# An attention and feed-forward layer on one core: the order of early loads, of one normalization and of the sums of Wq

## The chip, the core and the metric

The kernel runs on one core of a Trainium2 chip. A core has a matrix engine (TensorE, PE in the profile), three engines for elementwise work (VectorE or DVE, ScalarE or ACT, GpSimd or POOL) and SyncE (SP), which here only issues transfers. Each engine works off its own queue in order. A transfer is issued by an instruction in the queue of SP, ACT or POOL and then runs on 16 DMA engines that all queues share. The metric is the device time of one execution in microseconds (us).

## The reference

Everything is float32. There are 16 rows of a batch, each 128 by 1024.

```python
def layernorm(x):                       # over the last axis, no gain, no bias
    return (x - mean(x)) / sqrt(var(x) + 1e-5)

q = layernorm(x) @ Wq + bq              # 1024 -> 1024: 32 heads of 32
k = ctx @ Wk + bk                       # 1024 -> 256:  8 heads of 32
v = ctx @ Wv + bv                       # 1024 -> 256
w = softmax(q k^T / sqrt(32))           # four heads of q share one of k and v
x = x + (w v) @ Wo + bo                 # 1024 -> 1024
e = layernorm(x); e[:, 819:] *= -4      # the last fifth is inhibitory
out = x + scale * (e @ kernel)          # kernel: 1024 x 1024 of zeros and ones
```

## The kernel before, in words

**Groups and steps.** The 16 rows of the batch make 8 groups of two (`GB = 2`). A group's attention takes four steps; in a step `attend` (L761) issues the scores of one row and half of the heads as 32 small matmuls, and then for each of four tiles a maximum (`negm`, VectorE), four exponentials (ScalarE), a division (`inv` and `p`, VectorE), four transpositions (`tpp`, TensorE) and a copy (`pt`, ScalarE). At its end `weighted` (L606) multiplies by v. Between these parts TensorE works on the dense matmuls of the neighbouring groups.

**The order is written out by hand.** Under `tc.manual_schedule()` (L830) every instruction goes into its engine's queue in the order in which the program issues it. `Stream` (L23) makes this order: it keeps a clock `now`, a list of generators that issue dense work in pieces and tell how long each takes (about 0.85 us), and events that `later(us, fn)` puts at a time on that clock. `run` issues the events that are due, then the next piece. The clock is only the program's own reckoning; on the chip each instruction starts when its queue and its operands let it.

**Weights come in pieces.** Wq and Wo stay in memory and pass through a ring of eight pieces of 512 KB (`fetch`, L220). From the second group on, both products are made with seven block products in place of eight (`seven`, L462). They need four sums of blocks of Wq and four of Wo, which `combine` (L782) makes in place from the loaded pieces, one half of 128 by 512 at a time (L796), and stores to memory (L799); later fetches read them back. `spread` (L805) issues one sum every so many us of the clock. The sums of the second half of Wq and both halves of Wo run on GpSimd, those of the first half of Wq on VectorE.

**The start.** Ahead of the hand-written part the contexts of rows 0 and 1, Wv, Wk and the rows 0 and 1 of x are loaded (L186 to L191), the first ones over the queues of SP, ACT and POOL in turn. `load_by_quadrants` (L155) takes its queues in rotation; Wk is cut in two halves of four transfers, eight transfers of 128 KB in all. Then SP issues six pieces of Wq, the contexts of rows 2 and 3, two more pieces, the four blocks of Wo of `load_o_part(0)` (L816, issued at L823), and the rows 2 and 3 of x (`load_x`, L166, issued at L169). TensorE meanwhile makes v and k of the first group, transposes the normalized rows 0 and 1, and begins q with `plain(0)`, which uses the pieces as they are, without sums.

**Step one and two of the first group.** TensorE goes on with `plain(1)`, 16 pieces of q in four groups of four, during step one, and with k and v of the second group during step two. `norms(nxt, 8.5, 25.0)` puts the normalization of row 2 at 8.5 us and that of row 3 at 25.0 us on the stream's clock after the scores of step one. A normalization (`norm_x`, L387) is, on VectorE, two statistics (L283), their aggregate (L287), an addition (L289) and the scaling `xn` (L292), and between the last two one power on GpSimd (`rs_a`, L291). `between(gen, n, fn)` (L920) calls `fn` after the n-th piece of a generator; here it starts the sums of the first half of Wq, one every 1.5 us of the clock. `sums_of_wq(1)` starts those of the second half on GpSimd, one every 3.3 us. The four sums of Wo were started before step one (`sums_of_wo`, L867), also one every 3.3 us. When the last sum of a half is issued, its stores and four fetches follow on SP.

Of the kernel before, what the change touches and what calls it, by code (L numbers as in the profile page):

```python
# [76 lines left out]
def once(fn, *args):  # L77
    fn(*args)
    yield 0.0
# [3 lines left out]
def kernel(  # L83
# [71 lines left out]
    def load_by_quadrants(dst, w, queues, *cuts):  # L155

        src = w.rearrange("(k c f) n -> k f c n", k=NB, f=32)
        n = 0
        for lo, hi in zip((0,) + cuts, cuts + (NC,)):
            for k in range(NB):  # L160
                queues[n % len(queues)].dma_start(
                    out=dst[k * 32 : (k + 1) * 32, lo:hi], in_=src[k][:, lo:hi]
                )
                n += 1

    def load_x(b, tag="row"):  # L166

        x_t = work.tile([P, D], FP, tag=tag, name=f"xn{b}", bufs=2)
        nc.sync.dma_start(out=x_t, in_=x[b])  # L169
        xns[b] = x_t  # L170
# [11 lines left out]

    three = (nc.sync, nc.scalar, nc.gpsimd)
    load_ctx(0, three)  # L186
    load_by_quadrants(wv_sb, Wv, (nc.scalar, nc.gpsimd, nc.sync), 2, 4)
    load_ctx(1, three)
    load_by_quadrants(wk_sb, Wk, (nc.scalar, nc.gpsimd, nc.sync), 4)
    load_x(0)  # L190
    load_x(1)  # L191
    ident = const.tile([P, P], FP, name="ident")
# [27 lines left out]
    def fetch():  # L220
        n = len(pieces)
        if n < len(feed):
            t = work.tile([P, PIECE], FP, tag="piece", name=f"piece{n}", bufs=RING)
            src = feed[n]()
            nc.sync.dma_start(out=t.rearrange("p (c n) -> p c n", c=src.shape[1]), in_=src)
            pieces.append(t)
# [603 lines left out]
    with tc.manual_schedule():  # L830
        stream = Stream()

        at_q = {}
        for k in range(2):
            for o in range(2):
                for r in range(2):
                    at_q[r, o, k] = want(lambda r=r, o=o, k=k: q_block(r, o, k))
        qs, os = {1: prep_q(1)}, {}
        for grp in range(NGRP):
            os[grp] = out_proj(grp)  # L840
            if grp + 2 < NGRP:
                qs[grp + 2] = prep_q(grp + 2)

        for _ in range(RING - 2):
            fetch()
        for j in range(GB):
            load_ctx(GB + j)
        for _ in range(2):
            fetch()
        o_parts = [load_o_part(0)]  # L850
        for j in range(GB):
            load_x(GB + j, "turn")

        def plain(a):
            return prep_q_plain(a, {(r, k): at_q[r, a, k] for r in range(2) for k in range(2)})

        for j in range(GB):
            for h in range(2):
                turn_ctx(j, h)
            stream.add(prep_v(0, [j]))  # L860
        stream.add(prep_k(0))
        stream.run(0.0, lambda: len(stream.queue) > 1)
        nc.vector.tensor_scalar_mul(bqs, bqT, scale)
        for j in range(GB):
            norm_x(j)

        def sums_of_wo():  # L867
            def then():
                o_parts.append(load_o_part(1))

            stream.later(10.0, load_ffn)
            stream.later(8.0, lambda: spread(combine("o", 0, o_parts[0]), 3.3, then))

        stream.add(
            prep_x(0, 0),
            prep_x(0, 1),
            once(sums_of_wo),
            once(prep_ctx, 1, 7.0, 9.0, 11.0, 12.0),
            plain(0),
        )  # L880
        stream.run(0.0, lambda: stream.queue)

        def norms(grp, *us):
            for j in range(GB):
                stream.later(us[j], lambda j=j: norm_x(grp * GB + j))

        def get_x(grp):

            for j in range(GB if grp < NGRP else 0):
                b = grp * GB + j  # L890
                load_x(b, "turn")
                stream.later((10.0 if grp == 2 else 5.0) + 4.0 * j, lambda b=b: rows_x(b))

        def turn_rows(grp):
            for n, at in enumerate((30.0, 32.0, 34.0, 36.0)):
                stream.later(at, lambda n=n: turn_x(grp * GB + n // 2, n % 2))

        def get_ctx(grp):
            if grp < NGRP:
                for j in range(GB):  # L900
                    load_ctx(grp * GB + j)

        def residuals(grp):
            for j in range(GB):
                load_residual(grp * GB + j, 1.0 if grp == 0 else 4.0)

        def sums_of_wq(k):
            def then():
                for _ in range(4):
                    fetch()  # L910
                if k == 1:
                    spread(combine("o", 1, o_parts[1]), 3.3)

            part = {(r, o): pieces[at_q[r, o, k]] for r, o in BLOCKS}
            if k == 0:
                spread(combine("q", k, part, nc.vector), 1.5, then)
            else:
                spread(combine("q", k, part), 3.3, then)

        def between(gen, n, fn, *args):  # L920

            for i, us in enumerate(gen):
                yield us
                if i + 1 == n:
                    fn(*args)

        for grp in range(NGRP):
            b0, b1, nxt = grp * GB, grp * GB + 1, grp + 1
            p0, p1 = b0 - 2, b0 - 1
            first, more = grp == 0, nxt < NGRP  # L930
            last = grp == NGRP - 1
            length = 17.4 if first else 23.2 if grp < NGRP - 2 else 19.2
            if first:
                stream.add(
                    once(norms, nxt, 8.5, 25.0),
                    between(plain(1), 9, sums_of_wq, 0),
                    once(sums_of_wq, 1),
                    prep_k(nxt),
                    once(get_ctx, nxt + 1),
                    prep_v(nxt),  # L940
                    prep_x(nxt, 0),
                    prep_x(nxt, 1),
                    once(convert_ffn),
                    between(qs[nxt], 40, residuals, grp),
                )
            elif more:
                stream.add(
                    *([once(get_x, nxt), once(prep_ctx, nxt, 3.7, 8.0, 13.0, 18.0)] if grp == 1 else []),
                    once(turn_rows, nxt),
                    os[grp - 1],  # L950
                    once(get_ctx, nxt + 1),
                    prep_k(nxt),
                    once(load_residual, b0, 4.0),
                    prep_v(nxt),
                    qs[nxt],
                    once(get_x, nxt + 1),
                    once(prep_ctx, nxt + 1, 2.5, 7.0, 11.0, 16.0),
                )

                if nxt < NGRP - 1:  # L960
                    stream.add(ffn(p0), once(load_residual, b1, 2.0), ffn(p1))
            else:
                stream.add(
                    once(load_residual, p1, 1.0, "ctx"),
                    os[grp - 1],
                    once(load_residual, b0, 4.0, "ctx"),
                    ffn(p0 - 2),
                    once(load_residual, b1, 4.0),
                    ffn(p1 - 2),
                )  # L970
            if not more:
                for q in range(2 * NA):
                    b, a = grp * GB + q % GB, q // GB
                    start = stream.now
                    pts = attend(b, a, 15.0)
                    stream.later(15.0, lambda b=b, a=a, pts=pts: weighted(b, a, pts) or 1.0)
                    stream.run(start + 12.0)
                stream.run(stream.now, lambda: (b, a) not in yTs)
                break
            for q in range(2 * NA):  # L980
                b, a = grp * GB + q % GB, q // GB
                start = stream.now
                pts = attend(b, a, length)
                if q == 2 * NA - 1:
                    stream.run(start + length - 2.0, lambda: stream.queue)
                else:
                    stream.run(start + length - 2.0)
                stream.run(stream.now, lambda: None in pts)
                weighted(b, a, pts)
                stream.now += 1.0  # L990
        stream.add(
            os[NGRP - 1],
            ffn(B - 4),
            mixed(ffn(B - 3), ffn_transpose(B - 2), 10, 2),
            mixed(ffn(B - 2), ffn_transpose(B - 1), 8, 2),
            ffn(B - 1),
        )
        stream.drain()
# [49 lines left out]
```

## Time and profile before

| what | us |
|---|---|
| three timed runs | 785.81, 786.40, 787.71 (median 786.4) |
| the profiled execution | 785.56 |
| its span, first to last instruction | 783.8 |
| scores of step one, two, three begin | 41.58, 61.95, 80.50 |
| TensorE busy from 41.6 to 61.9 | 17.98 of 20.30 |
| TensorE busy from 61.9 to 80.5 | 18.11 of 18.60 |
| TensorE busy from 200 to 700 | 500 of 500 |
| TensorE idle before its first matmul | 7.01 |

The granted TensorE clock is 1.00 in all of these stretches. In a timeline a row gives the start, the duration, the engine, the line of the program, the operation, what it writes and reads, the shapes and the number of instructions that are merged in it; in brackets stands the idle time of the engine before it, and what ended it. A small q behind an engine's name (SPq, ACTq) is its queue issuing a transfer. Engines read ahead, so that a row can start a little before the one above it ends.

### The profile page before, as it was taken

The page shows a single profiled execution, that of the slowest core. Times are in us where ns is not written, and L with a number is a line of the kernel's source. Part 1 is how long each engine was busy: PE and PEld are TensorE (multiplying, and loading weights), DVE is VectorE, ACT ScalarE, POOL GpSimd, SP SyncE. Part 2 cuts the span into 40 slices and gives each one's busy share as a digit, 9 for nine tenths or more (in the row PEclk, how much of TensorE's full clock was granted, in tenths as well). Part 3 has the DMA queues.
Part 4 walks back from the last instruction along what each step waited for, and adds up shares of the span by engine and source line. Part 5 has one row for each costly group of instructions (what it writes and reads, how often), then busy time and mean ns, then how long its engine had stood idle before and what let it go on. Part 6 is the DMA issues. An engine that isn't in the chain of part 4 may idle for free.

```text
span 783.8 us, 13740 instructions
## 1 busy us (share of the span) xinstructions
PE 765.3 (98%) x5008; PEld 570.7 (73%) x5008; DVE 488.7 (62%) x887; ACT 323.1 (41%) x1261; POOL 114.6 (15%) x142
## 2 busy tenths in 40 slices
PE   5999999999999999999999999999999999999997
PEld 4877884689747986479855898558985689456476
DVE  1358648756766667466784667755676666765552
ACT  0244854435234453344433444344434445575100
POOL 4066502010100102020020200202001010103000
PEclk9999999999999999999999999999999999999999
DMA  9999899969698777878688795977769667763702
GB/s 241 317 332 316 327 342 372 271 196 304 236 299 237 235 237 233 293 215 262 222 270 264 192 290 207 307 230 206 265 216 313 207 199 235 253 202 103 264 27 81
DMA packets 99412, 192.42 MB, mean 245 GB/s; under 512 B 8256, under 2 KB 57728, under 8 KB 99344
## 3 DMA queue, kind: packets, MB, share of 16 engines
q1 hardware_dynamic: 97568, 189.30, 75.4%
q10 hardware_dynamic: 1248, 1.11, 0.6%
q0 software_dynamic: 528, 1.12, 0.6%
q8 instruction: 40, 0.66, 0.4%
q14 instruction: 28, 0.23, 0.1%
HBM read 161.09 MB, written 30.41 MB: 244 GB/s over the span
## 4 chain that ended last, share of the span: by engine, by line
PE 87%; DMA 6%; DVE 4%; POOL 1%; issue 1%; SPq 0%; ACT 0%; DVEq 0%; POOLq 0%
PE f L323 14%; PE o_u L662 13%; PE q_u L451 13%; PE o_v L662 7%; PE tpp L601 7%; PE q_v L451 7%; PE v L323 6%; PE k L323 5%; PE sc L568 4%; PE av L611 4%; PE q_c L451 3%; PE o_c L662 3%; DMA ctx<-in_ctx_dram 2%; DMA wo<-in_L_xattn_Wo_dram 1%; DMA piece<-in_L_xattn_Wq_dram 1%; POOL wo L796 1%
## 5 line engine op out<-in xcount | busy, mean ns | idle before, releaser
L584 ACT ACTIVATE p<-sc,negm 128x128 f32<-128x128 f32 x512 | 181.4, 369 | 133.2 <-DVE negm L580 73.1
L603 ACT COPY pt<-tpp 128x512 f32<-128x512 f32 x128 | 74.7, 591 | 146.8 <-PE tpp L601 146.5
L580 DVE TENSOR_REDUCE negm<-sc 128x4 f32<-128x512 f32 x128 | 86.8, 680 | 45.6 <-PE sc L568 45.6
L584 ACT ACTIVATION_READ_ACCUMULATOR p<-sc,negm 128x1 f32 x512 | 105.5, 206 | 0.0
L323 PE MATMUL f<-wf_sb,x2l 128*128 128x512 f32 x256 | 104.3, 407 | 0.0
L323 PE MATMUL f<-wf_sb,x2h 128*128 128x512 f32 x256 | 100.5, 393 | 0.0
L596 DVE TENSOR_TENSOR p<-p,inv 128x512 f32<-128x512 f32 x128 | 91.9, 718 | 4.4
L451 PE MATMUL q_u<-t,piece 128*128 128x128 f32 x672 | 81.3, 275 | 0.0
L601 PEld LDWEIGHTS tpp<-ident,p 128*128 128x128 f32 x512 | 61.9, 141 | 24.6 <-issue 16.7
L601 PE MATMUL tpp<-ident,p 128*128 128x128 f32 x512 | 75.9, 273 | 3.4 <-DVE p L596 3.2
L451 PEld LDWEIGHTS q_u<-t,piece 128*128 128x128 f32 x672 | 78.1, 192 | 0.1
L180 POOL TENSOR_TENSOR x<-x,bo_b 128x256 f32<-128x256 f32 x64 | 54.3, 874 | 154.7 <-DMA x<-in_x_dram 154.7
L323 PE MATMUL v<-wv_sb,cT 128*128 128x256 f32 x256 | 61.2, 388 | 9.5 <-DMA wv_sb<-in_L_xattn_Wv_dram 7.7
L662 PE MATMUL o_v<-piece,s 128*128 128x512 f32 x128 | 60.3, 598 | 0.5 <-DVE x L676 0.5
L662 PE MATMUL o_u<-piece,s 128*128 128x512 f32 x128 | 59.2, 594 | 0.6 <-DVE x L676 0.6
L323 PEld LDWEIGHTS v<-wv_sb,cT 128*128 128x128 f32 x256 | 47.8, 194 | 16.2 <-DVE cT L349 9.2
L662 PE MATMUL o_u<-piece,yT 128*128 128x512 f32 x128 | 58.6, 600 | 0.0
L323 PE MATMUL k<-cT,wk_sb 128*128 128x256 f32 x256 | 58.0, 380 | 0.0
L323 PEld LDWEIGHTS f<-wf_sb,x2l 128*128 128x128 f32 x256 | 48.2, 188 | 10.5 <-issue 1.1
L323 PEld LDWEIGHTS f<-wf_sb,x2h 128*128 128x128 f32 x256 | 48.2, 188 | 9.6 <-issue 0.5
L323 PEld LDWEIGHTS k<-cT,wk_sb 128*128 128x128 f32 x256 | 47.9, 190 | 8.8 <-issue 2.6
L568 PEld LDWEIGHTS sc<-kT,qT 32*128 32x128 f32 x1024 | 31.4, 186 | 25.7 <-issue 25.7
(86 smaller groups left out, 938.1 us busy)
## 6 DMA issues: line engine op xcount, KB each, us to landing
piece<-o SPq DMA_DIRECT2D x64, 512.0 KB, 4.6
piece<-q SPq DMA_DIRECT2D x56, 512.0 KB, 5.1
piece<-in_L_xattn_Wq_dram SPq DMA_DIRECT2D x50, 512.0 KB, 5.0
piece<-in_L_xattn_Wo_dram SPq DMA_DIRECT2D x48, 512.0 KB, 4.7
xn<-in_x_dram SPq DMA_DIRECT2D x16, 512.0 KB, 6.8
x<-in_x_dram SPq DMA_DIRECT2D x16, 512.0 KB, 5.1
ctx<-in_ctx_dram SPq DMA_DIRECT2D x60, 128.0 KB, 6.7
out_dram<-x SPq DMA_DIRECT2D x15, 512.0 KB, 2.7
```

The costliest lines, as they stand in the source:

```text
L180: lambda cut=cut: nc.gpsimd.tensor_add(x_t[:, cut], x_t[:, cut], bo_b[:, cut]) and None,
L323: nc.tensor.matmul(mm, lhsT=lhsT, rhs=rhs, start=k == 0, stop=k == n - 1)
L451: nc.tensor.matmul(mm if part is None else mm[:, part], lhsT=lhsT, rhs=rhs, start=start and n == k == 0, stop=k == len(some) - 1, skip_gro ...
L568: nc.tensor.matmul(tiles[i][:, g], lhsT=qT[rows, g], rhs=kT[rows, a, cols], start=True, stop=True,)
L580: nc.vector.tensor_reduce(negm, tile_, AX.X, ALU.max, negate=True)
L584: nc.scalar.activation(p[:, g], tile_[:, g], AF.Exp, bias=negm[:, g : g + 1], accum_out=total[:, g : g + 1],)
L596: nc.vector.tensor_mul(p, p, inv.unsqueeze(2).to_broadcast([P, NG, S]))
L601: nc.tensor.transpose(tp[:, g], p[:, g], ident)
L603: nc.scalar.copy(pt, tp)
L611: nc.tensor.matmul(mm[i * HD : (i + 1) * HD], lhsT=vs[b][:, h * HD : (h + 1) * HD], rhs=pts[i], start=True, stop=True,)
L662: nc.tensor.matmul(mm, lhsT=lhsT[:, 2 * k + c], rhs=w[:, c], start=start and k == c == 0, stop=k == c == 1, skip_group_check=True,)
L796: engine.tensor_tensor(dst[:, cols], left[:, cols], right[:, cols], op)
```

## The change

Three places are edited.

```diff
-    load_by_quadrants(wk_sb, Wk, (nc.scalar, nc.gpsimd, nc.sync), 4)
+    load_by_quadrants(wk_sb, Wk, (nc.sync, nc.scalar), 4)
...
         for _ in range(2):
             fetch()
+        load_x(GB, "turn")
         o_parts = [load_o_part(0)]
-        for j in range(GB):
-            load_x(GB + j, "turn")
+        load_x(GB + 1, "turn")
...
             if first:
                 stream.add(
-                    once(norms, nxt, 8.5, 25.0),
-                    between(plain(1), 9, sums_of_wq, 0),
+                    once(norms, nxt, 4.0, 25.0),
+                    between(plain(1), 12, sums_of_wq, 0),
                     once(sums_of_wq, 1),
                     prep_k(nxt),
```

- The eight transfers of Wk are issued by SP and ACT in turn, four each; before, ACT and POOL had three each and SP two.
- Row 2 of x is issued ahead of the four blocks of Wo, row 3 behind them as before.
- The normalization of row 2 is put at 4.0 us of the stream's clock after the scores of step one, in place of 8.5.
- The sums of the first half of Wq are started after the twelfth of the sixteen pieces of `plain(1)`, in place of the ninth.

No instruction is added or removed, and nothing is computed otherwise.

## The prediction

> **What bounds the kernel now.** I read the page first, then TensorE's timeline, then the queues that feed it. TensorE is busy for nearly the whole span, so only its gaps can be won, and anything that makes a gap longer is paid in full:
>
> ```profile
> PE 765.3 (98%) x5008; PEld 570.7 (73%) x5008; DVE 488.7 (62%) x887; ACT 323.1 (41%) x1261; POOL 114.6 (15%) x142
> ```
>
> The span is 783.8, so 18.5 us are idle. TensorE's timeline shows where, within the reach of the change (the number in brackets is idle time, with what ended it):
>
> ```profile
> 7.01 3.46 PE L323 MATMUL v<-wv_sb,cT 128*128 128x256 f32 x8 [7.01 <-DMA wv_sb<-in_L_xattn_Wv_dram]
> 14.95 3.72 PE L323 MATMUL v<-wv_sb,cT 128*128 128x256 f32 x16 [1.79 <-DVE cT L349]
> ...
> 52.72 0.60 PE L601 MATMUL tpp<-ident,p 128*128 128x128 f32 x4
> ...
> 59.53 0.63 PE L601 MATMUL tpp<-ident,p 128*128 128x128 f32 x4 [2.32 <-DVE p L596]
> ...
> 75.92 0.63 PE L601 MATMUL tpp<-ident,p 128*128 128x128 f32 x4 [0.49 <-DVE p L596]
> ```
>
> From 80 to 700 us there is hardly a gap: the change decides over steps one and two (41.6 to 80.5) and over the start. VectorE's timeline says what is late at 59.53: the last division of step one (58.10) stands behind the normalization of row 2 (53.34 to 56.52) and the first sum of Wq:
>
> ```profile
> 49.58 0.93 DVE L596 TENSOR_TENSOR p<-p,inv 128x512 f32<-128x512 f32 x1
> ...
> 53.34 1.27 DVE L283 BATCH_NORM_STATS2 st_a<-xn 128x6 f32<-128x512 f32 x2
> ...
> 55.71 0.81 DVE L292 TENSOR_SCALAR xn<-xn,mv_a,rs_a 128x1024 f32<-128x1024 f32 x1 [0.67 <-POOL rs_a L291]
> 56.43 1.29 DVE L796 TENSOR_TENSOR piece<-piece,piece 128x512 f32<-128x512 f32 x2
> ...
> 58.10 1.29 DVE L596 TENSOR_TENSOR p<-p,inv 128x512 f32<-128x512 f32 x1
> ...
> 72.34 1.75 DVE L292 TENSOR_SCALAR xn<-xn,mv_a,rs_a 128x1024 f32<-128x1024 f32 x1 [0.67 <-POOL rs_a L291]
> ```
>
> The normalization needs POOL once (rs_a). POOL's timeline shows that it does so after all eight halves of Wo's sums, which began only when Wo had landed:
>
> ```profile
> 41.85 2.50 POOL L796 TENSOR_TENSOR wo<-wo,wo 128x512 f32<-128x512 f32 x2 [17.19 <-DMA wo<-in_L_xattn_Wo_dram]
> 44.56 8.31 POOL L796 TENSOR_TENSOR wo<-wo,wo 128x512 f32<-128x512 f32 x6 [0.22 <-DMA wo<-in_L_xattn_Wo_dram]
> 55.12 0.55 POOL L291 TENSOR_TENSOR rs_a<-ve_a,minus_half 128x1 f32<-128x1 f32 x1 [2.25 <-DVE ve_a L289]
> ```
>
> And Wo is late because the transfers are full: the table by 2 us has a DMA share of 0.99 to 1.17 from 2 to 48 us.
>
> **Part one: row 2 ahead of Wo.** One more 512 KB transfer lands in front of Wo's four. Wo's second and fourth blocks released POOL at 41.85 and 44.56, two blocks apart: 1.35 us each. So POOL starts at 43.2, not 41.85. Row 2 itself (issued at 35.64, landed 10.1 later, at 45.7) would land at about 40.3; nobody needs it that early, so this wins nothing by itself. On SP the four issues of Wo go back by one issue (0.6); the transfers behind them keep their place.
>
> **Part two: the norm at 4.0 in place of 8.5.** I follow the source's own clock (a piece of 0.85, a step's first maximum 0.7 after the scores, then one every 2.4, a division 2.3 after each). The norm of row 2 then stands on VectorE after division 0 and before maximum 2. On POOL rs_a goes ahead of Wo's fourth sum instead of behind it. Walking the queues with the durations above (in brackets: before):
> - POOL: Wo's third sum ends at 51.3 (49.96, plus the 1.35).
> - VectorE: division 0 ends 48.9; statistics, mean and variance 1.7: ready at 50.6. rs_a waits for POOL until 51.3 and takes 0.55. Then xn: POOL starts Wo's fourth sum in the same moment, as at 72.3 before, where xn took 1.75 and not 0.81. So xn ends at 53.6.
> - Maximum 2 (0.68) ends 54.2, division 1 (0.17 and 0.95, POOL busy) 55.3. TensorE wanted it at 52.72 and gets it at 55.4: a new stall of 2.7.
> - What queues behind: ScalarE's exponentials 2 (1.47) run to 55.7, its share of q's copy to 56.1; VectorE's share of that copy, which waits for ScalarE's, to 56.4, maximum 3 to 57.0, division 2 to 57.8; TensorE has it at 57.9, 0.3 late. Exponentials 3, a copy of pt and the next copy of q run to 59.5, division 3 to 60.6, TensorE at 60.7 (59.53).
>
> So step one ends 1.2 **later**: the 2.32 at the fourth transposition goes, and 2.7, 0.3 and 0.6 come. With POOL free and xn at 0.81, tpp 1 would come at 53.8 and the fourth at about 59.4: even then only 0.2 is won, as the norm's 3.2 us sit ahead of maximum 2 instead of behind division 2.
>
> The rule on this is in the Trainium skill, "SBUF — State Buffer", section "Who interferes with whom": VectorE and GpSimd share one pair of ports as an exclusive lock; two-input operations and tensor_scalar in a two-port mode take it, reductions do not. The rows at 55.71 and 72.34 agree for xn; by the rule as by the row it is 1.75, without the lock 0.81, and tpp 1 would come at 54.4. The rule also lets the statistics run free beside POOL; no row here tests that.
>
> That the statistics run at 0.64 a half beside POOL no row shows; the bounds are 0 and one POOL half of 1.27 each. rs_a waits 0.7 for POOL anyway, so 0 to 1 us; I take 0, since the maxima, also of one input, keep 0.68 in the same window.
>
> **Part three: the sums of Wq three pieces later.** One of four sums stays in step one, behind division 3; three go into step two, in place of one. There they meet POOL's own sums of Wq (61.1 to 66.3 before), where a half took 3.16 / 2 = 1.6 instead of 0.65. Walk: first sum 60.5 to 64.0, second 64.1 to 67.3, maximum 0 at 67.2 (65.06), third sum, maximum 1, division 0, fourth sum to 71.7, maximum 2, division 1 to 73.1, the norm of row 3 from 73.0 (69.96), xn ends 77.1, maximum 3, division 2 at 78.8. TensorE wants it at 76.4 and gets it at 78.9 (75.92): +3.0. If VectorE wins one more race for the port it is 78.3: +2.4. The same walk on the kernel before hits its step one to 0.1 but puts this point at 76.86, 0.94 too late; against itself it says +1.4 to +2.0. Bounds +1.4 and +3.0; I take the middle, **+2.2**.
>
> On SP the four stores of these sums wait for VectorE, and behind them stand four loads of Wq (landed 70.7 to 76.5, needed from 83.92), the next context and the stores of POOL's sums. They go back by 2 to 6.6 us, and TensorE by 2.2. The loads still have 4 us. The sums' way back through memory had 1.5 us (landed at 90.03, TensorE at 91.51): cover, but thin.
>
> **Part four: Wk by SP and ScalarE's queue.** Three transfers leave POOL, two go to SP, one to ScalarE. Gain: context 1 (landed 14.06) shares the engines with fewer others, at most the 1.79 of TensorE's wait. Loss: row 0 was issued at 11.76 behind two Wk issues that took 3.29 on SP; behind four it may land up to 2 us later, and its norm feeds TensorE at 25.41. Neither reaches the sum: the walk of step one begins with Wo's landing and POOL. With TensorE 0.7 or 1.3 earlier at 41.6 its end is the same, with 1.5 later 0.6 more. POOL's own small loads come 1.65 earlier; nobody waits. I take 0; bounds 0 and +0.6. The cover is the stall at POOL: without it, the start's gain would show.
>
> **Sum.** 0 (start) + 1.2 (step one) + 1.0 (step two) = +2.2, carried to the end since TensorE has no gap to absorb it. The profiled execution took 785.56: 787.8. It is 0.84 under the median of 786.4: **788.6**.
>
> **Rivals.**
> - *Faster.* The norm finds POOL free: Wo lands no later, POOL's third sum ends by about 49, the port isn't contended. Both stalls go (2.32 + 0.49), and some 0.3 of the start shows: 786.4 - 3.1 = 783.3. For it: VectorE is idle from 43.5 to 46.8 and again 0.76 at 50.5. Against: the norm cannot start before division 0 in its queue, and Wo sits in a full stream. It decides if tpp 1 stays at 52.7. Chance 0.10.
> - *Absorbed.* Wo lands with less delay (0 in place of 1.35: step one then ends 0.4 later) and the races for the port go VectorE's way: 786.4 and up to 1 either way. Chance 0.25. For it: my walk is too late once on the kernel before.
> - *A new wait on the sums.* The stores on SP go back 6 us, and the sums of Wq miss TensorE at the first product that uses them (q_u from t, 91.51 before, then about 93.7). At up to 2 us late: 788.6 + 2 = 790.6. For it: the chain of waits runs through these stores and loads at 61.8 to 71.8. Against: 1.5 us of cover. Chance 0.13.
> - *My forecast*, 787.2 to 789.8: chance 0.52.
>
> **How the numbers follow.** A measurement of this kernel can tell about 0.3%, 2.36 us: the bounds are 784.0 and 788.76. My own case lies across the upper one, some 0.29 of its 0.52 above; with most of the third rival, slower is 0.42, and I add 0.03 for losses I have not seen: 0.45. Faster: 0.10. Same: 0.45. The likeliest case alone spans 787.2 to 789.8; the range for 8 in 10 takes in the absorbed case and the late sums, 785.3 to 790.8, leaving out the fast rival.
>
> **What would show it.** Right: a stall at the second transposition of step one, ended by p; rs_a on POOL between Wo's third and fourth sums; xn at about 1.75; POOL's first sum of Wo near 43.2; three sums of Wq after step two's scores; the third transposition of step two 1.4 to 3 us later. Wrong: the second transposition at 52.7, POOL starting at 41.9, or gaps that appear after 90 us.

## The result, and the profile after

| | before | after |
|---|---|---|
| median of 22 runs each, us | 787.12 (785.72 to 789.50) | 788.14 (787.13 to 789.96) |
| ratio to before, 95% interval | | 1.0017 (1.0010 to 1.0024) |
| profiled execution, its span | 785.56, 783.8 | 788.58, 786.8 |
| scores of step one, two, three begin | 41.58, 61.95, 80.50 | 41.23, 64.32, 83.71 |

The change costs about 1 us: small, but the interval leaves out 1. The two profiles lie 3.0 apart, more than the medians, because the profile of before is a low execution of its kernel (below all 22 runs of the table) and that of after a slightly high one. The granted clock has a part in it: it stayed at 1.00 in the profile of before and fell to 0.50 for 3.4 us in that of after (last section). So the traces are read for the order of things and for single durations; sizes of effects come from the ratios over many runs.

The engines' busy time in the page of after says that the work is the same (5008 matmuls), but that they took 2.1 us longer:

```profile
PE 767.4 (98%) x5008; PEld 572.2 (73%) x5008; DVE 487.1 (62%) x887; ACT 322.7 (41%) x1261; POOL 111.9 (14%) x139
```

TensorE's timeline of after, at the places shown of before. The 7.01 and 1.79 of the start are 7.30 and 1.38. In step one the stall has moved from the fourth transposition (2.32) to the second (3.46) and has grown; in step two it is 1.33 in place of 0.49. The row of q below takes 3.04 for 8 matmuls; at 60.20 the next 8 take 1.89:

```profile
7.30 5.91 PE L324 MATMUL v<-wv_sb,cT 128*128 128x256 f32 x16 [7.30 <-DMA wv_sb<-in_L_xattn_Wv_dram]
14.60 3.72 PE L324 MATMUL v<-wv_sb,cT 128*128 128x256 f32 x16 [1.38 <-DVE cT L350]
...
49.35 0.60 PE L602 MATMUL tpp<-ident,p 128*128 128x128 f32 x4
...
56.00 1.09 PE L602 MATMUL tpp<-ident,p 128*128 128x128 f32 x4 [3.46 <-DVE p L597]
56.88 3.04 PE L324 MATMUL q<-xT,piece 128*128 128x256 f32 x8
...
61.93 0.60 PE L602 MATMUL tpp<-ident,p 128*128 128x128 f32 x4
...
79.12 0.63 PE L602 MATMUL tpp<-ident,p 128*128 128x128 f32 x4 [1.33 <-DVE p L597]
```

POOL's timeline of after: the sums of Wo begin at 43.80 (41.85 before), and rs_a goes in between the third and the fourth with no idle time in front of it:

```profile
43.80 2.49 POOL L797 TENSOR_TENSOR wo<-wo,wo 128x512 f32<-128x512 f32 x2 [19.48 <-DMA wo<-in_L_xattn_Wo_dram]
46.51 5.39 POOL L797 TENSOR_TENSOR wo<-wo,wo 128x512 f32<-128x512 f32 x4 [0.22 <-DMA wo<-in_L_xattn_Wo_dram]
51.86 0.55 POOL L292 TENSOR_TENSOR rs_a<-ve_a,minus_half 128x1 f32<-128x1 f32 x1
52.38 2.93 POOL L797 TENSOR_TENSOR wo<-wo,wo 128x512 f32<-128x512 f32 x2
```

VectorE's timeline of after: the variance is ready at 49.95, the scaling waits 2.49 for POOL, takes 1.74 instead of 0.81, and the division for the second transposition (54.91) stands behind it. Further down, three of the four sums of Wq lie in step two (64.10, 67.49, 70.57), and the scaling of row 3 (75.56) with its 1.75 is ahead of the division at 78.02:

```profile
48.25 1.27 DVE L284 BATCH_NORM_STATS2 st_a<-xn 128x6 f32<-128x512 f32 x2
...
52.44 1.74 DVE L293 TENSOR_SCALAR xn<-xn,mv_a,rs_a 128x1024 f32<-128x1024 f32 x1 [2.49 <-POOL rs_a L292]
...
54.91 0.95 DVE L597 TENSOR_TENSOR p<-p,inv 128x512 f32<-128x512 f32 x1
...
64.10 2.87 DVE L797 TENSOR_TENSOR piece<-piece,piece 128x512 f32<-128x512 f32 x2
...
67.49 1.75 DVE L797 TENSOR_TENSOR piece<-piece,piece 128x512 f32<-128x512 f32 x2
...
70.57 1.28 DVE L797 TENSOR_TENSOR piece<-piece,piece 128x512 f32<-128x512 f32 x2
...
75.56 1.75 DVE L293 TENSOR_SCALAR xn<-xn,mv_a,rs_a 128x1024 f32<-128x1024 f32 x1 [0.67 <-POOL rs_a L292]
...
78.02 0.95 DVE L597 TENSOR_TENSOR p<-p,inv 128x512 f32<-128x512 f32 x1
```

Step three begins 3.21 later than before, the span ends 3.0 later: nothing more is lost, and little given back, behind 83.7.

### The profile page after: what moved, and what is told of

Its sections match the earlier page's. It is cut to its first block, busy times and chain, and to the rows that moved or that the text cites. A ratio compares the mean times of both kernels' runs of the same rounds, so it can differ in the third digit from the quotient of the medians.

```text
span 786.8 us, 13741 instructions
## 1 busy us (share of the span) xinstructions
PE 767.4 (98%) x5008; PEld 572.2 (73%) x5008; DVE 487.1 (62%) x887; ACT 322.7 (41%) x1261; POOL 111.9 (14%) x139
## 4 chain that ended last, share of the span: by engine, by line
PE 86%; DMA 7%; DVE 3%; POOL 2%; issue 1%; SPq 0%; ACT 0%; ACTq 0%; DVEq 0%; POOLq 0%
PE f L324 14%; PE o_u L663 13%; PE q_u L452 13%; PE tpp L602 7%; PE o_v L663 7%; PE q_v L452 7%; PE v L324 6%; PE k L324 5%; PE sc L569 4%; PE av L612 4%; PE q_c L452 3%; PE o_c L663 3%; DMA piece<-in_L_xattn_Wq_dram 2%; DMA ctx<-in_ctx_dram 2%; DMA wo<-in_L_xattn_Wo_dram 1%
```

## The experiments

Twelve kernels ran. Each ratio is to runs of the kernel before on the same chip in the same session; in brackets its 95% interval. A ratio is not the quotient of the two medians; where they differ much, both are given. "Fourth" is the fourth transposition of step one, "third" the third of step two (before: 59.53 and 75.92).

### One part of the change alone

The norm of row 2 at 4.0:

```diff
-                    once(norms, nxt, 8.5, 25.0),
+                    once(norms, nxt, 4.0, 25.0),
```

> The normalization of row 2 at 4.0 in place of 8.5, and nothing else. Theory (POOL holds it): on POOL the power rs_a stands between Wo's third and fourth sums and cannot start before the third ends, near 50.0; xn meets the fourth sum at the port and takes about 1.75; the second transposition of step one comes near 54.6 instead of 52.7, the fourth near 60.5 instead of 59.5, and the kernel is 1 to 2 us slower than before. Rival (the lateness is the sums of Wq, the early norm is harmless): the second transposition stays at 52.7, the stall at the fourth goes, and the kernel is about 2 us faster.

Measured: 788.53, ratio **1.0037** (1.0021 to 1.0052): the whole loss, from one number. How large it is, is less sure: by the ratio 2.9 us, by the medians 1.4 (787.15 before), with three of the 12 runs at 791.4 to 793.6. Fourth at 61.77, third at 78.36, and a new stall of 2.49 at the second transposition (55.72). But the cause is only half the one that was named. TensorE's, POOL's and VectorE's timelines of this kernel, and behind them the division's row of before:

```profile
55.72 0.63 PE L601 MATMUL tpp<-ident,p 128*128 128x128 f32 x4 [2.49 <-DVE p L596]
```

```profile
44.38 4.94 POOL L796 TENSOR_TENSOR wo<-wo,wo 128x512 f32<-128x512 f32 x4 [0.21 <-DMA wo<-in_L_xattn_Wo_dram]
51.57 0.55 POOL L291 TENSOR_TENSOR rs_a<-ve_a,minus_half 128x1 f32<-128x1 f32 x1 [2.25 <-DVE ve_a L289]
```

```profile
48.07 1.80 DVE L596 TENSOR_TENSOR p<-p,inv 128x512 f32<-128x512 f32 x1
49.79 1.27 DVE L283 BATCH_NORM_STATS2 st_a<-xn 128x6 f32<-128x512 f32 x2
...
52.16 1.75 DVE L292 TENSOR_SCALAR xn<-xn,mv_a,rs_a 128x1024 f32<-128x1024 f32 x1 [0.66 <-POOL rs_a L291]
```

```profile
47.91 0.92 DVE L596 TENSOR_TENSOR p<-p,inv 128x512 f32<-128x512 f32 x1
```

Here POOL was idle for 2.25 and waited for VectorE, so its queue did not hold rs_a back. The norm is late because its statistics stand behind a division that took 1.80 beside POOL's sums (0.92 before; 0.69 to 1.80 over the kernels here), and its scaling took 1.75 beside the next sum. All of it stands in front of the next maximum.

The sums of Wq after the twelfth piece:

```diff
-                    between(plain(1), 9, sums_of_wq, 0),
+                    between(plain(1), 12, sums_of_wq, 0),
```

> The sums of the first half of Wq three pieces later, and nothing else. Theory (the norm is what costs): division 3 no longer stands behind the first sum, so that the fourth transposition of step one comes near 57.7 instead of 59.5; the sums in step two give about half of it back at the third transposition there; the kernel is about 1 us faster than before, 0 to 2. Rival (the sums are what costs, since three of them meet POOL's own sums at the port in step two): the third transposition of step two is 2 us or more later than before's 75.9, and the kernel is 1 to 2 us slower.

Measured: 786.17, ratio 0.9993 (0.9980 to 1.0007): no effect that can be told. TensorE's timeline of this kernel shows why: what is won at the fourth (1.58 earlier than before) is given back at the third, where a stall of 1.75 stands in place of 0.49.

```profile
57.95 0.63 PE L601 MATMUL tpp<-ident,p 128*128 128x128 f32 x4 [0.81 <-DVE p L596]
...
75.59 0.63 PE L601 MATMUL tpp<-ident,p 128*128 128x128 f32 x4 [1.75 <-DVE p L596]
```

Wk by two queues, and row 2 ahead of Wo:

```diff
-    load_by_quadrants(wk_sb, Wk, (nc.scalar, nc.gpsimd, nc.sync), 4)
+    load_by_quadrants(wk_sb, Wk, (nc.sync, nc.scalar), 4)
```

> Wk over the queues of SP and ACT only, and nothing else. Theory: TensorE reaches step one some 0.3 us earlier, as in the changed kernel (41.23 against 41.58), while Wo lands some 0.6 later; the stall at the fourth transposition keeps its size, so that 0 to 0.5 us is won or nothing. Rival (the start is what costs): Wo lands later, and the kernel is 1 us or more slower.

Measured: 786.67, ratio 1.0000 (0.9988 to 1.0012). Step one's scores begin at 40.92 instead of 41.58, and the fourth transposition comes at 58.94, still after a stall of 2.38: 0.59 of the lead is left there. It is lost behind it, where TensorE's clock falls to half (0.50 in the last column but two of the third row, which is a window of the trace) and step two begins at 62.58, not 61.95; the third comes at 76.45.

```profile
58.94 0.63 PE L601 MATMUL tpp<-ident,p 128*128 128x128 f32 x4 [2.38 <-DVE p L596]
...
62.58 1.52 PE L568 MATMUL sc<-kT,qT 32*128 32x128 f32 x32
```

```profile
60.00:61.00 1.00, 1.00 (x6) 0.27 (x9) 1.00 (x2) 0.37 (x2) 0.13 (x1) 0.50 0.78 264
```

```diff
+        load_x(GB, "turn")
         o_parts = [load_o_part(0)]
-        for j in range(GB):
-            load_x(GB + j, "turn")
+        load_x(GB + 1, "turn")
```

> Row 2 of x loaded ahead of Wo's blocks, and nothing else. Theory: POOL's first sum of Wo starts 1.35 later, near 43.2, and its last ends near 54.2, still ahead of rs_a at 55.1, so that TensorE's times do not move: within 0.5 us of before. Rival (Wo's delay costs by itself): the fourth transposition of step one comes 1 us or more later than 59.5.

Measured: 787.44, ratio 1.0012 (1.0001 to 1.0023), some 0.9 us by the ratio and 0.3 by the medians, at the edge of what can be told. POOL began at 42.73 (41.85 before), the fourth came at 60.48, the third at 76.86. In this execution the scores began 0.65 later than before too, so its rows do not say how much is Wo's delay.

### The change with one part undone

> The changed kernel with row 2 behind Wo's blocks again. Theory: Wo lands 1.35 earlier than in the changed kernel, so POOL's third sum ends near 50.5 and rs_a waits hardly at all; the stall at the second transposition falls from 3.46 to about 2.2, short enough that the clock stays up; the kernel is 1 to 1.5 us faster than the changed one, about as slow as before or up to 0.5 slower. Rival (POOL's hold does not matter, only the place in VectorE's queue): within 0.5 us of the changed kernel.

Row 2 behind Wo again: 786.93, ratio 1.0003 (0.9995 to 1.0012). POOL begins at 41.56, and rs_a comes at 50.24 after 0.57 of idle time. The second transposition is at 54.39 with a stall of 2.48, the fourth at 59.57, the third at 77.21. Row 2's place is thus worth 0.0014 in the company of the other parts (1.0017 to 1.0003) and 0.0012 alone.

> The changed kernel with the normalization of row 2 at 8.5 again. Theory: the second transposition is on time (52.4), the fourth comes near 58.8; the kernel is 2 to 3 us faster than the changed one and 0 to 1 faster than before. Rival (the late sums of Wq are what costs): as slow as the changed kernel.

The norm at 8.5 again, the other three parts kept: 785.38, ratio **0.9978** (0.9969 to 0.9986). Undoing this one number wins 0.0039 over the full change, as much as it lost alone (0.0037). The remaining three parts are together a little faster than before, which none of them shows by itself. A part of that is the clock: among the runs of this comparison the mean granted clock was below 0.999 in 12 of 29 runs of before and in 2 of 12 of this kernel. Among the other runs the medians are 786.24 and 785.38, 0.9 apart instead of 1.3. No single row explains the rest, and the one profile of this kernel (785.76) cannot show an effect of this size.

> The changed kernel with the sums of the first half of Wq after the ninth piece again. Theory (the late sums help, above all beside the early norm): the first sum stands ahead of division 2 and 3 again, and the kernel is 0.5 to 1.5 us slower than the changed one. Rival (the late sums are a part of the loss): 0.5 us or more faster than the changed one.

The sums after the ninth piece again: 787.93, ratio 1.0008 (0.9996 to 1.0020), against 1.0017 for the full change. The intervals overlap: the later sums cost nothing that can be told, here as alone. Stall at the second transposition 2.78, fourth 60.79, third 77.41.

### Moving the norm to where both its queues are free

VectorE and POOL are both idle shortly before step one. If the norm is dear only because of what stands beside it, it should cost nothing there. Row 2 is loaded two pieces earlier, and its norm is issued before step one (row 3's stays at 25.0):

```diff
+        load_x(GB, "turn")
         for _ in range(2):
             fetch()
         o_parts = [load_o_part(0)]
-        for j in range(GB):
-            load_x(GB + j, "turn")
+        load_x(GB + 1, "turn")
...
             stream.later(10.0, load_ffn)
+            stream.later(10.0, lambda: norm_x(GB))
...
-            for j in range(GB):
-                stream.later(us[j], lambda j=j: norm_x(grp * GB + j))
+            stream.later(us[1], lambda: norm_x(grp * GB + 1))
```

> The kernel before, with row 2 loaded ahead of the last two pieces of Wq and its normalization issued ahead of step one, between the transpositions of the contexts, and ahead of Wo's sums on POOL. Theory (a norm costs only where its queues are wanted; here VectorE waits for contexts and POOL for Wo): xn takes 0.81, the four transpositions of step one are on time, the fourth near 57.2; both stalls by p shrink from 2.8 together to 0 to 1.4; the kernel is 1.4 to 2.8 us faster than before. Rival (any earlier norm or any delay of Wo and of the pieces of Wq costs): as slow as before or slower.

Measured: 785.05, ratio 0.9981 (0.9969 to 0.9993). No stall is left in step one: the fourth comes at 56.85. Step two takes 2.08 back at the third (75.13). The same with the sums after the twelfth piece:

> The same, and the sums of the first half of Wq three pieces later. Theory: the first step as in the kernel without the late sums; the late sums keep the port away from POOL's own sums in step one and meet it in step two; within 1 us of the one without them, 1.5 to 3 us faster than before. Rival (late sums push division 2 of step two): a stall of 2 us or more at the third transposition of step two, no gain over before.

Measured: **784.25**, ratio **0.9965** (0.9953 to 0.9977; five runs), the fastest of all kernels here. All five runs had a mean granted clock of 0.999 or more; against the 17 of the 29 runs of before compared with it that had it too (median 786.24), the gain is 2.0 us. Its TensorE, VectorE and POOL rows: the scaling takes its uncontended 0.81, before POOL has any sum to make, and step one has no stall:

```profile
57.58 0.60 PE L601 MATMUL tpp<-ident,p 128*128 128x128 f32 x4
...
74.77 0.63 PE L601 MATMUL tpp<-ident,p 128*128 128x128 f32 x4 [1.33 <-DVE p L596]
...
91.21 0.68 PE L451 MATMUL q_u<-t,piece 128*128 128x128 f32 x4 [0.69 <-DMA piece<-q]
```

```profile
40.20 0.81 DVE L292 TENSOR_SCALAR xn<-xn,mv_a,rs_a 128x1024 f32<-128x1024 f32 x1 [0.66 <-POOL rs_a L291]
```

```profile
39.62 0.55 POOL L291 TENSOR_TENSOR rs_a<-ve_a,minus_half 128x1 f32<-128x1 f32 x1 [14.44 <-DVE ve_a L289]
43.53 2.49 POOL L796 TENSOR_TENSOR wo<-wo,wo 128x512 f32<-128x512 f32 x2 [3.37 <-DMA wo<-in_L_xattn_Wo_dram]
```

### Both norms ahead of step one

The next step would be to take row 3's norm, which stands in front of the third transposition's division, out of step two as well (sums after the twelfth piece):

```diff
+        for j in range(GB):
+            load_x(GB + j, "turn")
         for _ in range(2):
             fetch()
         o_parts = [load_o_part(0)]
-        for j in range(GB):
-            load_x(GB + j, "turn")
...
             stream.later(10.0, load_ffn)
+            stream.later(10.0, lambda: norm_x(GB))
+            stream.later(10.0, lambda: norm_x(GB + 1))
...
-                    once(norms, nxt, 8.5, 25.0),
```

> The kernel before, with rows 2 and 3 of x both loaded ahead of the last two pieces of Wq, both normalizations ahead of step one and of Wo's sums on POOL, and the sums of the first half of Wq three pieces later. Theory (the stall left in step two, 1.3 to 2.1 us, comes from the norm of row 3 and its 1.75 at the port): it goes, no transposition of steps one and two waits over 0.5 us, and the kernel is about 1 us faster than with row 2 alone, 3 to 4 us faster than before. Rival (two more rows ahead of Wo and two pieces make POOL's sums or TensorE wait): no faster than with row 2 alone.

Measured: 786.72, ratio 1.0002 (0.9987 to 1.0018): the gain of the run before is gone. TensorE's timeline shows two waits, the second for sums that come back from memory too late:

```profile
73.10 0.63 PE L601 MATMUL tpp<-ident,p 128*128 128x128 f32 x4 [1.67 <-DVE p L596]
...
92.94 0.68 PE L451 MATMUL q_u<-t,piece 128*128 128x128 f32 x4 [1.67 <-DMA piece<-q]
```

and POOL's and VectorE's why. Without row 3's rs_a, POOL makes all eight halves in one go, and VectorE's fourth sum meets them at the port (3.43 for two halves, 1.28 in after):

```profile
57.97 12.62 POOL L796 TENSOR_TENSOR piece<-piece,piece 128x512 f32<-128x512 f32 x8 [1.75 <-PE q L323]
```

```profile
67.71 3.43 DVE L796 TENSOR_TENSOR piece<-piece,piece 128x512 f32<-128x512 f32 x2
```

> The same, and Wk over the queues of SP and ACT only. Theory: with no stall left in steps one and two to absorb it, TensorE's earlier start (0.3 to 0.7) shows: 0 to 0.7 us faster than with Wk over three queues. Rival: the start's gain is only the spread of single profiles, and the two are the same.

The same with Wk by two queues: 786.77, ratio 0.9998 (0.9983 to 1.0012), 0.05 us from the run without. Waits of 1.95 (72.16) and 0.24 (92.00). Step two's scores began 1.37 earlier than in the run without (58.75, 60.12), step three's 0.48 later: the lead went into the wait of 1.95 and a clock that halved behind it. Wk's queues are worth nothing here that can be told.

> Both early rows and both normalizations ahead of step one as in the run with both, but the sums of Wq again after the ninth piece. Theory (VectorE's late sums, meeting GpSimd's eight unbroken halves in step two, and their late way back cost that run its gain): the four sums end near 64.4 as with one early row, the second transposition of step two stands at 70.7 or earlier without a stall, the third near 73 without the 2.08 of that run, no wait for piece at q_u, scores of step three near 78; median 783.2, ratio 0.995 to 0.997. Rival (GpSimd's eight unbroken halves hold the port whatever VectorE's sums do, or the two rows at the front delay the last pieces of Wq): a stall of over 1 us stays in step two or comes before 50 us, median 785 to 787, ratio 0.998 or more.

The sums after the ninth piece again: 786.41, ratio 0.9988 (0.9975 to 1.0002). The wait at q_u is gone, so it was the late sums. The theory's gain did not come, and the rival's mark (a stall of over 1 us in step two) did: VectorE's last three sums now lie in one stretch to 66.67, almost all of it beside POOL's eight halves (57.90 to 70.25), and the first maximum of step two stands behind them.

```profile
57.61 5.72 DVE L796 TENSOR_TENSOR piece<-piece,piece 128x512 f32<-128x512 f32 x4
63.25 0.34 DVE L442 TENSOR_SCALAR qT<-q,bqs 128x128 f32<-128x128 f32 x1
63.51 3.16 DVE L796 TENSOR_TENSOR piece<-piece,piece 128x512 f32<-128x512 f32 x2
66.60 1.27 DVE L580 TENSOR_REDUCE negm<-sc 128x4 f32<-128x512 f32 x2
```

```profile
70.95 0.63 PE L601 MATMUL tpp<-ident,p 128*128 128x128 f32 x4 [2.41 <-DVE p L596]
71.41 4.44 PE L323 MATMUL v<-wv_sb,cT 128*128 128x256 f32 x12
```

Left to try, and not tried: the sums of Wq on POOL and VectorE in turn rather than side by side.

## Why the prediction came out as it did

**The total.** 788.6 was forecast and 788.14 measured. The shift was +2.2 by the sum and is +1.0 by the medians (interval +0.8 to +1.9, from the ratio). Its starting point, the median of three runs, was 0.7 below the median of 22; that made up for part of what the sum had too much. That the total came so close is partly luck in another way too: the 2.2 was 1.2 for the norm and 1.0 for the late sums, and the runs give the norm more and the late sums nothing.

**The mechanism of step one: right.** The marks named in advance are there: a stall at the second transposition (forecast 2.7, measured 3.46), rs_a between Wo's third and fourth sums, xn at 1.74, statistics that run free beside POOL (1.27 for two halves, the open price taken at 0).

**"Part one": right.** POOL's start was put at 43.2, 1.35 late; it came at 43.80 in after. One execution says little here: with row 2 right in front of Wo the four profiles have 42.54, 42.73, 43.53 and 43.80, with Wo at its old place the five (before among them) have 41.23 to 41.85. The means, 43.15 and 41.52, are 1.6 apart. By the ratios row 2's place costs some 1 us (0.0012 alone, 0.0014 undone), the first with an interval that nearly touches 1.

**"Part two": the largest error.** Its +1.2 for step one's end hung on POOL: Wo late by 1.35, so rs_a late. The norm alone costs 1.4 us by the medians and 2.9 by the ratio (1.0037), with Wo at its old place and POOL idle, and undoing it alone in the full change wins 2.3 by the medians (each against its before) and 3.1 by the ratios (0.0039). The prediction had a sentence for this case, "even then only 0.2 is won", with the second transposition at 53.8 and the fourth at about 59.4. With the norm alone they came at 55.72 and 61.77. The sentence let the scaling run at 0.81, and that met POOL's next sum (1.75), as the division ahead of the norm met the one before (1.80 for 0.92). These two are 1.8 of the 1.9 at the second transposition. A pause of POOL when rs_a is wanted is not a free port around it.

Here the rule that was weighed in advance bears once more: row and rule agree that xn and the division are slowed beside POOL, and by the Trainium skill, "SBUF — State Buffer", section "Who interferes with whom", the engine that issues first keeps the shared pair for its whole instruction. It would explain why the same division has anything from 0.69 to 1.80 over these kernels; that it is the order of issue was not tested by itself.

**"Part three": wrong in size, right in place.** The third transposition of step two was put at 78.3 to 78.9 and came at 79.12; three sums lie in step two; the stores' way back had cover, TensorE did not wait for it. But the cost that the sum gives to it, +1.0, is not there: later sums alone are 0.9993 (0.9980 to 1.0007), and undoing them gives 1.0008 against 1.0017. The gain at the fourth transposition and the loss at the third cancel. In after, the third is late mainly because step one ended late.

**"Part four": right in its number, its reason not shown.** Taken at 0; measured 1.0000 (0.9988 to 1.0012), and 0.05 us in a second pair. The cover was named as the stall at POOL. But with Wk alone POOL began 0.58 earlier too (41.27), and the lead passed the stall and was lost when the clock halved. The mean granted clock was below 0.999 in 11 of the 12 runs of that kernel and in 21 of the 35 of before compared with it, so a small gain may be hidden there (the medians are 0.5 apart); that stays open.

**Not in the sum at all.** TensorE's clock halved after the new stall (last section). With POOL's start and TensorE's measured, the same walk of the queues gives 55.99 and 61.32 for the second and fourth transpositions; measured are 56.00 and 61.93. The 0.6 between is about what the clock leaves of it: from the second to the fourth it is 5.18 with row 2 undone, where the clock stayed at 1.00, and 5.93 to 6.05 in the three kernels in which it halved there (after, norm alone, sums undone). It is not what decides the median of after: six of its 22 runs had a mean clock of 1.0, and they (787.30 to 789.96) were not faster than the rest. In the kernel before it does weigh (last section).

**The rivals.** "Faster" asked for a norm that finds POOL and port free; the change did not do that, but the kernels that put the norm before step one did, and reached 784.25 where the rival had 783.3. "A new wait on the sums" did not come in the changed kernel; it came, with the late sums, 0.69 long when one norm was taken out of the way and 1.67 when both were.

The parts do not add up: the four alone sum to 0.0042, together they are 0.0017. With a stall that moves from one transposition to the next, each part's price depends on which wait ends last. What stays open is why the three parts without the norm are faster than before (0.9978) also in the runs whose clock stayed up.

## What to carry to other kernels

When a step that alternates between two engines is moved, look for a place where both queues and the port between them are free, not for an earlier time: the same normalization cost 1.4 us (medians) to 2.9 us (ratio) at 4.0, and ahead of the step it won some 1.5 us, 2.8 with the later sums (both by the ratio). Price each operation of a moved step by its duration beside its new neighbours (0.81 or 1.75), and its neighbours by theirs. And follow a removed stall to the next place that is late: here each kernel that cleared step one of stalls had 1.33 to 2.41 in step two, where before had 0.49.

## What the runs showed of the hardware

**The clock can halve after a stall that seems short.** The windows of after: the last column but two is the granted clock. It fell just as TensorE resumed at 56.00, and the matmuls there took 1.09 for 0.60:

```profile
52.50:56.00 3.50, 0.04 (x1) 0.03 (x1) 3.32 (x4) 1.18 (x7) 2.81 (x2) 0.97 0.76 302
56.00:57.00 1.00, 1.00 (x5) 1.00 (x6) 0.39 (x2) 1.00 (x4) 0.00 (x0) 0.50 0.86 336
...
59.00:60.00 1.00, 1.00 (x7) 0.86 (x6) 0.12 (x1) 0.85 (x4) 0.00 (x0) 0.90 0.85 250
```

In the last experiment it fell after a stall of 2.41:

```profile
71.00:72.00 1.00, 1.00 (x6) 0.90 (x7) 0.96 (x3) 0.51 (x3) 1.00 (x1) 0.83 0.85 294
72.00:73.00 1.00, 1.00 (x4) 0.81 (x3) 1.00 (x2) 1.00 (x7) 1.00 (x2) 0.50 1.02 348
...
75.00:76.00 1.00, 1.00 (x7) 0.87 (x6) 0.00 (x0) 0.24 (x2) 1.00 (x2) 0.96 1.01 342
```

From the partial slices, the halved stretch runs from 55.79 to 59.20 in the one and from 71.66 to 75.08 in the other: 3.4 us both times. The length of a stall alone does not decide. The clock fell after 1.95 (both norms early, Wk by two queues), 2.04 (norm undone), 2.38 (Wk alone), 2.49 (norm alone) and 2.78 (sums undone) as well; it did not fall after 2.08 (norm ahead of step one), 2.32 (before), 2.48 (row 2 undone) and 2.61 (row 2 alone).

What decides is how much of a stall lies inside one window of 3.413 us. In the clock records of the fourteen traces the first rise to 1.00 lies between 10.04 and 12.16, and each of the seven falls ahead of the kernel's end comes a whole number of such windows behind it (13, 14 or 18) and lasts one. In windows laid from that rise to 775 us, over 3000 of them, TensorE is idle for 1.95 us or more in seven, and these are the seven ahead of the falls; no other has more than 1.91. The smallest of the seven, with the window behind it, and below them a stall of 2.08 that an edge at 73.24 cut into 0.19 and 1.89 (the second figure is the window's length, the third TensorE's busy time):

```profile
69.95:73.36 3.41, 1.46 (x10) 1.15 (x9) 3.34 (x7) 2.46 (x11) 3.41 (x4) 1.00 0.68 216
73.36:76.78 3.42, 3.42 (x12) 2.76 (x11) 2.65 (x4) 2.08 (x10) 3.42 (x3) 0.50 1.05 348
```

```profile
73.24:76.66 3.42, 1.53 (x9) 1.45 (x10) 3.12 (x7) 2.46 (x10) 3.42 (x3) 1.00 1.12 256
76.66:80.07 3.41, 3.41 (x32) 2.04 (x34) 0.43 (x2) 0.77 (x2) 3.33 (x5) 1.00 1.13 258
```

So the same stall can halve the clock in one execution and not in the next. The kernel before, with its stall of 2.32, shows it: in four sessions the mean granted clock was below 0.999 in 60 of its 110 runs, and by the medians of each session these took 1.1 to 1.9 us longer than the others. An estimate from the figures above: if the edges lie anywhere, a stall of 2.32 has 1.91 to 1.95 us in one window in 54 to 56% of the cases; 60 of 110 is 55%.

The Trainium skill, "TensorE: Matmul & The Clock Gate", section "What's actually happening", has the clock halved after at least one idle window of some 3.4 us that runs freely, not from the kernel's start. The traces agree with the window: the halved stretch is 3.4 us, the falls lie on one grid, and equal stalls end differently. But no window here was idle as a whole (3.24 us at most, in after), and by the runs 1.95 us of idle time in one were enough.

**The start varies by itself.** In kernels whose start is unchanged, the scores of step one began between 41.42 and 41.74, where only a later load or norm was moved between 41.38 and 42.25, and with Wk on two queues between 40.43 and 41.23. An earlier start of about 1 us is real, and no ratio shows it: what two of the traces show is that a later wait and the half clock took it.
